# Graph network on one core: gate terms in column quarters, a reordered last finish, a later transpose

## The chip, the cores and the metric

The kernel runs on one core of one Trainium2 chip. The metric is device time in microseconds (us): the median of the runs of one launch. A core has a matrix engine (TensorE, in the profile PE, its weight loads PEld), a vector engine (VectorE, DVE), a scalar engine (ScalarE, ACT), GpSimd (POOL) and a queue that only issues transfers (SyncE, SP). Every engine takes its own instructions in order, and semaphores tie the engines together. TensorE writes its results to PSUM, which has 8 banks here; everything else lies in SBUF or in DRAM.

## The reference

A graph of 2708 nodes with 512 features each, an adjacency matrix `adj` (2708 x 2708), and four layers, each ending with `x = layernorm(x + layer(x))`. What matters for the change are the gates of layer 1 and the whole of layer 3:

```python
# layer 1: two gates per node, each from the summed and the own features
type_sum = adj @ x
attn_a = sigmoid(concatenate([type_sum, x], 1) @ Wa.T + ba)   # one number per node
attn_b = sigmoid(concatenate([type_sum, x], 1) @ Wb.T + bb)
x_b = adj @ (x @ W_gcnb) + b_gcnb                              # = type_sum @ W_gcnb + b_gcnb
...
x = layernorm(x + sigmoid(attn_a * x_a + attn_b * x_b))
# layer 2: out = x @ w0 + A x @ w1 + A^2 x @ w2 + A^3 x @ w3, worked out in three hops
# layer 3, with deg the count of neighbours
a_norm = deg**-0.5 * (adj + eye) * deg**-0.5
x = layernorm(x + relu((a_norm @ x + x) @ W + b))
```

All is float32. In this program one float32 matrix product of 128 rows by 128 columns appears in the profile as two matmul instructions, called passes here.

## The kernel before

The product of the adjacency with the features is done seven times (one "sweep" each: layer 0, the two products of layer 1, the three hops of layer 2, layer 3). Each sweep forms 2 x 2 blocks with seven products instead of eight (Strassen's scheme in Winograd's form), so VectorE adds and subtracts blocks of adjacency and features ahead of TensorE, and adds products from PSUM into tiles of results behind it. The results lie transposed: features on the 128 partitions, nodes along the free dimension. `C[h, c]` (layers 0 and 1) or `cc(s, c)` (layers 2 and 3) is such a tile: half `h` of the nodes, a quarter `c` of the features (`DC` = 4 quarters of 128 features). In the sweeps of layers 0 and 1 the nodes of a half are cut into four ranges of 384, 384, 256 and 330 nodes (`RANGES`); in the others into two ranges of two parts each, `s` = 0 and 1, of 338 or 339 nodes (`RANGES2`).

The order of the work is written as a list of events. `at(pos, fn)` puts a piece of work at a position, and the list is sorted by position and emitted (L1344); a scheduler of the framework then places the instructions on the engines, mostly in that order, and adds the semaphores. An event made with `hold=True` is tied to stay behind what stands before it on its engine. In layer 1 one position unit is one product of a range: 10 blocks of 128 rows for two column halves, 40 passes. In the last sweeps two position units are seven products (`u = 2 / 7`).

Behind each completed range a "finish" runs between the matmuls of the next product:

- `done1` (L912), layer 1, called once for each half of each range, 8 times in all, with `p0` the position of its start. For each tile of up to 128 nodes (22 in all: 20 of 128, two of 74) event `b` first takes the two gate terms: four matmuls with 128 nodes of `C` as weights and the 128 x 2 gate weights `wab_sb` as moving data (L917), an addition on VectorE (L919), a sigmoid on ScalarE (L920). Then come the dense product with `W[1]` (helper `dense`, L586, 8 passes of 512 columns), the bias, the gate and the store.
- `done5` (L1263), the third hop of layer 2: `b` turns a tile of nodes back with TensorE (L1232), normalises it (`layernorm`, L539) and stores it; `c`, 0.85 positions later, turns the normalised tile once more (L581), ScalarE copies it from PSUM into one of two `xT` tiles (L583), and GpSimd stores it (L601) for layer 3.
- `done6` (L1298), layer 3, called for two ranges and two halves. `pre(s, c)` (L1310) does three VectorE operations over a whole part of results (L1313 to L1315), which need a row of degrees (`rows`, L1299) and a tile from DRAM (`load_x3T`, L1305). Then for each of the 6 tiles of nodes `a` fetches the node's features (`fetch2`, GpSimd's queue, into one of the 6 `nat` tiles) and `b` does the dense product, bias and relu (L1332, L1333), the layernorm and the store. The last of the four calls is range 1, half 0, which ends the kernel.

`layernorm` goes from engine to engine: statistics on VectorE (L541, L543, L545), a power on GpSimd (L546), a product on VectorE (L548), the scaling on ScalarE (L551). GpSimd also issues most of the loads and stores of features, in the same queue as its powers. The adjacency, the row tiles, the degree rows and the `x3T` tiles share one ring of 38 tiles of SBUF (`RING`).

Where the last 84 rows of both halves are multiplied (`rest`, L456 and L1201), the kernel already cuts the array into four groups of 32 rows and runs four matmuls of 32 rows each, one in every group (L468, L1210).

Of the kernel before, what the change touches and what calls it, by code (L numbers as in the profile page):

```python
# [21 lines left out]
F32 = mybir.dt.float32  # L22
BF = mybir.dt.bfloat16
AF = mybir.ActivationFunctionType
ALU = mybir.AluOpType
P = 128
# [42 lines left out]
def gnn_kernel(ctx: ExitStack, tc: tile.TileContext, x, adjT, w_sa, a_sa, w_gcn, b_gcn, wab, bab, w_hop, w_out,  # L69
# [32 lines left out]
    nc.vector.memset(rdeg, 1.0)  # L102
    wab_sb = const.tile([P, 2 * DC, 2], F32, name="wab_sb")
    bab_sb = const.tile([P, 2], F32, name="bab_sb")
    vmat = const.tile([P, DC, 4], F32, name="vmat")
# [647 lines left out]
    def start0():  # L753
# [10 lines left out]
        for c in range(DC):  # L764
            nc.vector.tensor_copy(vmat[:, c, 2:4], wab_sb[:, DC + c, :])

    def x0_load(k, s):
# [22 lines left out]
    W = {}  # L790
# [120 lines left out]

    def done1(p0, dp, last, R0, n, h, C, tiles):  # L912
        for i, (t, lo, w) in enumerate(tiles):
            def b(t=t, lo=lo, w=w):
                pz = bank("pz", [P, 2])
                for c in range(DC):
                    nc.tensor.matmul(pz[:w], C[h, c][:, lo : lo + w], wab_sb[:, c, :], start=c == 0,  # L917
                                     stop=c == DC - 1)
                nc.vector.tensor_tensor(gate[:w, t, :], pz[:w], gate_x[:w, t, :], ALU.add)  # L919
                nc.scalar.activation(gate[:w, t, :], gate[:w, t, :], AF.Sigmoid)  # L920
                px = dense(lambda c: C[h, c][:, lo : lo + w], W[1], w)
                y = nat("y")
                nc.vector.tensor_tensor(y[:w], px[:w], vec[1][:w], ALU.add)
                nc.scalar.mul(y[:w], y[:w], gate[:w, t, 1:2])
                move(nc.gpsimd, XB[t], y[:w])

            at(p0 + 0.25 + dp * i, b)
# [335 lines left out]
    def done5(p0, dp, g, i0, n, h, cc, tiles):  # L1263
        for i, (s, lo, w) in enumerate(tiles):
# [13 lines left out]
            at(p, b)  # L1278
            at(p + 0.85, c)

# [17 lines left out]
    def done6(p0, dp, g, i0, n, h, cc, tiles):  # L1298
# [4 lines left out]
        x3T = {}  # L1303

        def load_x3T(s, c):  # L1305
            t = ring_tile("x3T")
# [10 lines left out]
        for s in range(2):  # L1317
            at(p0 - 0.6, lambda s=s: rows(s))
            for c in range(DC):
                at(p0 - 0.5 + 0.4 * s + 0.05 * c, lambda s=s, c=c: load_x3T(s, c))  # L1320
                at(p0 + 0.4 * s + 0.05 * c, lambda s=s, c=c: pre(s, c), True)
        for i, (s, lo, w) in enumerate(tiles):
            got = {}
# [12 lines left out]

            p = p0 + 0.4 + (0.25 if dp > 0.13 else 0.15) * i
            at(p - 0.6, a)
# [58 lines left out]
```

## Time and profile before

| | |
|---|---|
| device time, median of 3 | 2927.45 us (2926.04 to 2929.18) |
| span of the profiled execution | 2926.3 us |
| TensorE busy | 98% of the span |
| VectorE busy | 76% |
| ScalarE, GpSimd busy | 20%, 23% |
| share of the chain that ended last: TensorE | 84% |
| the gate terms, `pz` L917 | from 519.8 to 897 us |
| second transposes of the last range of hop 3, `ps_t` L581 | 2521.6 to 2541.8 us |
| last matmul of the sweep of layer 3, then the last finish | 2892.6 us to the end |

In the timeline a row has the start, the duration, the engine, the line, the operation with its output and inputs, the weights' and the moving operand's shapes, a count of merged instructions and, in brackets, how long the engine was idle before and what ended that. Durations of matmuls overlap each other, because they are pipelined: what one costs is read from the distance of the starts. So the share of TensorE's busy time says that there is hardly any gap, and the gaps themselves are read in the table of waits.

### The profile page before, as it was taken

The page shows a single profiled execution, that of the slowest core. Times are in us where ns is not written, and L with a number is a line of the kernel's source. Part 1 is how long each engine was busy: PE and PEld are TensorE (multiplying, and loading weights), DVE is VectorE, ACT ScalarE, POOL GpSimd, SP SyncE. Part 2 cuts the span into 40 slices and gives each one's busy share as a digit, 9 for nine tenths or more (in the row PEclk, how much of TensorE's full clock was granted, in tenths as well). Part 3 has the DMA queues.
Part 4 walks back from the last instruction along what each step waited for, and adds up shares of the span by engine and source line. Part 5 has one row for each costly group of instructions (what it writes and reads, how often), then busy time and mean ns, then how long its engine had stood idle before and what let it go on. Part 6 is the DMA issues. An engine that isn't in the chain of part 4 may idle for free.

```text
span 2926.3 us, 37538 instructions
## 1 busy us (share of the span) xinstructions
PE 2866.8 (98%) x10914; PEld 1856.8 (63%) x10914; DVE 2234.4 (76%) x5667; ACT 571.5 (20%) x1121; POOL 661.3 (23%) x1178
## 2 busy tenths in 40 slices
PE   7999999999999999999999999999999999999998
PEld 5655665557765656866666666666666666665664
DVE  5898797666656675775789788887888878689886
ACT  4544200000145454651100000000000201101001
POOL 0133224213310101123213033030330413512212
PEclk9999999999999999999999999999999999999999
DMA  7666476444544333564667667576775766866652
GB/s 224 187 212 180 133 224 215 131 153 150 173 128 131 115 116 97 169 196 149 207 205 222 203 201 233 160 215 197 217 223 148 229 200 184 240 181 182 180 163 87
DMA packets 376250, 523.99 MB, mean 179 GB/s; under 512 B 64454, under 2 KB 326640, under 8 KB 376044
## 3 DMA queue, kind: packets, MB, share of 16 engines
q1 hardware_dynamic: 305688, 370.70, 43.4%
q0 software_dynamic: 53376, 139.76, 14.7%
q10 hardware_dynamic: 16980, 11.13, 1.3%
q8 instruction: 87, 1.43, 0.2%
q14 instruction: 119, 0.97, 0.1%
HBM read 432.14 MB, written 89.21 MB: 178 GB/s over the span
## 4 chain that ended last, share of the span: by engine, by line
PE 84%; DVE 6%; issue 4%; DMA 3%; POOL 1%; SPq 1%; ACT 0%; POOLq 0%; DVEq 0%; ACTq 0%
PE accu L1135 11%; PE accd L1135 11%; PE accc L1135 11%; PE ps_d L592 9%; PE accd L444 9%; PE accu L444 8%; PE accc L444 8%; PE acca L1135 5%; PE acca L444 4%; PE accr L1206 2%; DVE z L1095 1%; PE accr L1210 1%; PE accd L453 1%; PE ps_t L581 1%; PE pz L917 1%
## 5 line engine op out<-in xcount | busy, mean ns | idle before, releaser
L1095 DVE TENSOR_TENSOR z<-z 128x339 f32<-128x339 f32 (+1 forms) x966 | 456.3, 503 | 13.5 <-PE accu L1135 2.5
L1153 ACT COPY q<-accu 128x338 f32<-128x338 f32 (+1 forms) x84 | 34.3, 444 | 994.5 <-PE accu L1135 836.0
L1135 PE MATMUL accc<-s,t 128*128 128x338 f32 (+1 forms) x644 | 200.1, 455 | 0.0
L1135 PE MATMUL accu<-z,t 128*128 128x338 f32 (+1 forms) x644 | 194.9, 448 | 1.6 <-DVE q L1159 1.6
L1135 PE MATMUL accc<-z,t 128*128 128x338 f32 (+1 forms) x644 | 194.4, 448 | 0.0
L1135 PE MATMUL accd<-z,t 128*128 128x338 f32 (+1 forms) x644 | 193.6, 448 | 0.0
L546 POOL TENSOR_TENSOR rstd<-rstd,neg_half 128x1 f32<-128x1 f32 (+3 forms) x92 | 62.2, 676 | 579.3 <-DVE rstd L545 578.6
L1256 POOL DMA_DIRECT2D Y<-y x192 | 105.1, 554 | 373.6 <-DVE y L1251 344.2
L389 DVE TENSOR_TENSOR a<-a,a 128x384 f32<-128x384 f32 (+2 forms) x330 | 161.3, 509 | 19.5 <-PE accu L444 18.6
L1135 PEld LDWEIGHTS accc<-s,t 128*128 128x128 f32 x644 | 122.1, 192 | 65.9 <-issue 10.3
L1135 PEld LDWEIGHTS accd<-z,t 128*128 128x128 f32 x644 | 122.2, 190 | 61.3 <-issue 1.7
L1135 PEld LDWEIGHTS accu<-z,t 128*128 128x128 f32 x644 | 121.4, 190 | 62.0 <-DVE q L1159 2.1
L1135 PEld LDWEIGHTS accc<-z,t 128*128 128x128 f32 x644 | 121.7, 190 | 60.9 <-issue 2.2
L1095 DVE TENSOR_TENSOR s<-z 128x338 f32<-128x338 f32 (+1 forms) x322 | 150.0, 503 | 10.6 <-PE accc L1135 6.2
L1159 DVE TENSOR_TENSOR q<-q,accd 128x338 f32<-128x338 f32 (+1 forms) x112 | 56.2, 502 | 132.4 <-PE accd L1135 132.3
L953 ACT ACTIVATE e<-row,neg_s 128x384 f32<-128x384 f32 (+5 forms) x176 | 100.4, 571 | 89.9 <-DVE e L955 28.2
L955 DVE TENSOR_TENSOR e<-e,f 128x384 f32<-128x384 f32 (+5 forms) x176 | 87.3, 504 | 23.8 <-ACT f L954 23.0
L954 ACT ACTIVATE f<-row,neg_s 128x384 f32<-128x384 f32 (+5 forms) x176 | 100.1, 568 | 25.5 <-PE accc L444 6.2
L882 DVE SCALAR_TENSOR_TENSOR deg<-a,deg 128x384 f32<-128x384 f32 (+2 forms) x152 | 74.0, 502 | 30.8 <-DMA a<-in_adjT 30.2
L592 PE MATMUL ps_d<-w,q 128*128 128x512 f32 (+2 forms) x192 | 86.4, 595 | 4.7 <-DVE q L1315 3.4
L392 POOL DMA_DIRECT2D As<-a x120 | 65.0, 544 | 111.5 <-DVE a L389 103.6
L956 DVE SCALAR_TENSOR_TENSOR a<-a,e 128x384 f32<-128x384 f32 (+2 forms) x160 | 80.0, 506 | 3.7 <-DMA a<-in_adjT 1.3
(602 smaller groups left out, 5934.9 us busy)
## 6 DMA issues: line engine op xcount, KB each, us to landing
z<-As SPq DMA_DIRECT2D x320, 169.5 KB
z<-As SPq DMA_DIRECT2D x320, 169.0 KB
a<-in_adjT SPq DMA_DIRECT2D x240, 192.0 KB
z<-in_adjT SPq DMA_DIRECT2D x240, 169.5 KB
z<-in_adjT SPq DMA_DIRECT2D x240, 169.0 KB
a<-in_adjT SPq DMA_DIRECT2D x120, 165.0 KB
a<-in_adjT SPq DMA_DIRECT2D x112, 128.0 KB
As<-a POOLq DMA_DIRECT2D x60, 192.0 KB, 3.4
```

What stands on the lines that cost most here:

```text
L389: nc.vector.tensor_tensor(A[r, dst, k][:, :n], A[r, a, k][:, :n], A[r, b, k][:, :n], op)
L392: nc.gpsimd.dma_start(out=SD[m][k * P : (k + 1) * P, R0 : R0 + n], in_=A[r, dst, k][:, :n])
L444: nc.tensor.matmul(B[home, c][:, :n], X[STAT[p], k][:, c * P : (c + 1) * P], A[r, MOV[p], k][:, :n], start=bool(start and k == k0), stop=k ...
L592: nc.tensor.matmul(o, lhs(c), r, start=c == 0 and n == 0, stop=c == DC - 1, skip_group_check=True)
L882: nc.vector.scalar_tensor_tensor(d[:w, :n], a[:w, :n], 0.0, d[:w, :n], ALU.not_equal, ALU.add)
L953: nc.scalar.activation(e[:w, :n], row[R0, h][0][:w, :n], AF.Exp, bias=neg_s[:w, t : t + 1])
L954: nc.scalar.activation(f[:w, :n], row[R0, h][1][:w, :n], AF.Exp, bias=neg_s01[:w, t : t + 1])
L955: nc.vector.tensor_tensor(e[:w, :n], e[:w, :n], f[:w, :n], ALU.min)
L956: nc.vector.scalar_tensor_tensor(a[:w, :n], a[:w, :n], 0.0, e[:w, :n], ALU.not_equal, ALU.mult)
L1095: nc.vector.tensor_tensor(d[:, :n], Z[x + (k,)][:, :n], Z[y + (k,)][:, :n], op)
L1135: nc.tensor.matmul(B[home][:, :n], stat(v, k), a[:, :n], start=bool(start and k == 0), stop=k == nk - 1, skip_group_check=True)
L1256: nc.gpsimd.dma_start(out=rows[:, :, f * P : (f + 1) * P], in_=o[32 * f : 32 * (f + 1), : m * P].rearrange("p (b d) -> p b d", d=P))
```

## The change

There are three parts.

1. Gates of a range at once. Per call of `done1`, four matmuls take the four feature quarters of the whole range as moving data, each with 32 columns of weights (`wab_pad`, of which two are not zero), and each writes another group of 32 partitions of one bank `pg`: four quarters of the array's columns. ScalarE copies the bank into a tile `zg` of the ring. For each tile of nodes one matmul with 128 columns of `zg` as weights and a 128 x 2 matrix `pick` of zeros and ones adds the four quarters up. It comes after the dense product instead of before it, and the tiles of a range share one bank `pz`. `wab_pad` and `pick` are filled once.
2. In `done5` the second transpose comes 1.1 instead of 0.85 positions after the first.
3. In the last call of `done6` rows, loads and the `pre` work start earlier, during the last product (the features `c` >= 2, which are complete first, ahead of the others; part 1 ahead of part 0), the three tiles of part 1 come ahead of those of part 0, and the first dense product stands directly behind the last matmul of the sweep instead of 0.5 positions later. It is meant to let TensorE go on without waiting for the last results.

```diff
+    wab_pad = const.tile([P, DC, 32], F32, name="wab_pad")
+    nc.vector.memset(wab_pad, 0.0)
+    pick = const.tile([P, 2], F32, name="pick")
+    nc.vector.tensor_copy(pick, ident[:, 0:2])
+    for c in range(1, DC):
+        nc.vector.tensor_tensor(pick, pick, ident[:, 32 * c : 32 * c + 2], ALU.add)
...
+            nc.vector.tensor_copy(wab_pad[:, c, 0:2], wab_sb[:, c, :])
...
     def done1(p0, dp, last, R0, n, h, C, tiles):
+        Z = {}
+
+        def gates():
+
+            pg = bank("pg")
+            for c in range(DC):
+                nc.tensor.matmul(pg[32 * c : 32 * c + 32, :n], wab_pad[:, c, :], C[h, c][:, :n], start=True, stop=True)
+            Z[0] = trans("zg")
+            nc.scalar.copy(Z[0][:, :n], pg[:, :n])
+
+        at(p0 + 0.05, gates)
         for i, (t, lo, w) in enumerate(tiles):
-            def b(t=t, lo=lo, w=w):
-                pz = bank("pz", [P, 2])
-                for c in range(DC):
-                    nc.tensor.matmul(pz[:w], C[h, c][:, lo : lo + w], wab_sb[:, c, :], start=c == 0,
-                                     stop=c == DC - 1)
+            def b(i=i, t=t, lo=lo, w=w):
+                px = dense(lambda c: C[h, c][:, lo : lo + w], W[1], w)
+                if i == 0:
+                    Z[1] = bank("pz", [P, 8])
+                pz = Z[1][:, 2 * i : 2 * i + 2]
+                nc.tensor.matmul(pz[:w], Z[0][:, lo : lo + w], pick, start=i == 0, stop=True, skip_group_check=True)
                 nc.vector.tensor_tensor(gate[:w, t, :], pz[:w], gate_x[:w, t, :], ALU.add)
                 nc.scalar.activation(gate[:w, t, :], gate[:w, t, :], AF.Sigmoid)
-                px = dense(lambda c: C[h, c][:, lo : lo + w], W[1], w)
...
-            at(p + 0.85, c)
+            at(p + 1.1, c)
...
+        end = (g, h) == (1, 0)
...
-            at(p0 - 0.6, lambda s=s: rows(s))
+            at(p0 - (1.9 if end else 0.6), lambda s=s: rows(s))
             for c in range(DC):
-                at(p0 - 0.5 + 0.4 * s + 0.05 * c, lambda s=s, c=c: load_x3T(s, c))
-                at(p0 + 0.4 * s + 0.05 * c, lambda s=s, c=c: pre(s, c), True)
-        for i, (s, lo, w) in enumerate(tiles):
+                if end:
+                    a = p0 - 1.8 + 0.05 * c
+                    b = p0 - 1.5 + 0.2 * (c - 2) + 0.4 * s if c >= 2 else p0 + {
+                        (1, 1): -0.9, (1, 0): -0.6, (0, 1): -0.3, (0, 0): -0.07}[s, c]
+                else:
+                    a, b = p0 - 0.5 + 0.4 * s + 0.05 * c, p0 + 0.4 * s + 0.05 * c
+                at(a, lambda s=s, c=c: load_x3T(s, c))
+                at(b, lambda s=s, c=c: pre(s, c), True)
+        for i, (s, lo, w) in enumerate(tiles[3:] + tiles[:3] if end else tiles):
...
-            p = p0 + 0.4 + (0.25 if dp > 0.13 else 0.15) * i
+            p = p0 - 0.095 + 0.14 * i if end else p0 + 0.4 + 0.25 * i
             at(p - 0.6, a)
             at(p, b)
```

## The prediction

> **What bounds the kernel now.** I began with the page, to see which engine fills the span.
>
> ```profile
> PE 2866.8 (98%) x10914; PEld 1856.8 (63%) x10914; DVE 2234.4 (76%) x5667; ACT 571.5 (20%) x1121; POOL 661.3 (23%) x1178
> ```
>
> TensorE is idle for only 2926.3 - 2866.8 = 59.5 us. So there are two ways to gain: fewer passes, or one of these few gaps. Next I asked who TensorE waits for while layer 1 makes its gates (480 to 910 us):
>
> ```profile
> PE ps_r L840 <- DVE rcol L835: 1.3, 1, 1.3
> ```
>
> This is the whole answer: in these 430 us TensorE is the bound, and a pass taken away there shortens the kernel by its length. Its timeline gives the lengths:
>
> ```profile
> 512.07 0.59 PE L468 MATMUL accc<-r,B22R 32*128 32x384 f32 x2
> 512.08 0.59 PE L468 MATMUL accu<-r,B22R 32*128 32x384 f32 x2
> 512.49 0.49 PE L468 MATMUL accc<-r,B22R 32*128 32x384 f32 x2
> 512.50 0.49 PE L468 MATMUL accu<-r,B22R 32*128 32x384 f32 x2
> 512.92 4.14 PE L444 MATMUL accd<-a,B22A 128*128 128x384 f32 x12
> 516.90 0.72 PE L896 MATMUL ds<-ones_f,deg 128*128 128x1 f32 x6
> ...
> 520.15 0.50 PE L917 MATMUL pz<-wab_sb,C 128*128 128x2 f32 x4
> 520.51 0.59 PE L917 MATMUL pz<-wab_sb,W 128*128 128x2 f32 x4
> 520.96 1.96 PE L592 MATMUL ps_d<-w,C 128*128 128x512 f32 x4
> 522.76 1.88 PE L592 MATMUL ps_d<-w,W 128*128 128x512 f32 x4
> 524.47 2.74 PE L444 MATMUL accd<-a,B22C 128*128 128x384 f32 x8
> 527.05 0.50 PE L917 MATMUL pz<-wab_sb,C 128*128 128x2 f32 x4
> ```
>
> Starts count, not durations. The last two rows: 8 passes of 384 columns take 2.58 us. A tile's gates and dense product take 524.47 - 520.15 = 4.32 us; a dense product alone takes 3.43 (so in the chain of waits), hence a tile's gates 0.89, 0.11 for each of their 8 passes of only two columns. The L468 rows are four matmuls on row quarters, two passes each: all four first passes start within 0.01 us, all second ones 0.42 later.
>
> Then the end. TensorE from the last product on:
>
> ```profile
> 2891.30 1.30 PE L1135 MATMUL acca<-z,B21D 128*128 128x339 f32 x4
> 2894.84 13.14 PE L592 MATMUL ps_d<-w,q 128*128 128x512 f32 x30 [2.24 <-DVE q L1315]
> 2908.87 3.70 PE L592 MATMUL ps_d<-w,q 128*128 128x512 f32 x8 [0.89 <-DVE q L1315]
> 2912.83 4.56 PE L592 MATMUL ps_d<-w,q 128*128 128x512 f32 x10 [0.27 <-DVE q L1315]
> ```
>
> Three times it waits for `pre`. VectorE's waits from 2839 to 2893 us, and the busy times (PE, PEld, DVE, ACT, POOL) of the last 23 us of the sweep:
>
> ```profile
> DVE rstd L548 <- POOL rstd L546: 8.8, 6, 4.4
> ```
>
> ```profile
> 2870.00:2880.00 10.00, 9.34 (x33) 5.89 (x31) 4.16 (x12) 1.53 (x2) 6.10 (x12) 1.00 0.48 138
> 2880.00:2893.00 13.00, 11.67 (x40) 7.52 (x40) 7.06 (x17) 0.09 (x1) 4.86 (x10) 1.00 0.41 125
> ```
>
> VectorE has room (11.2 of 23 us used), but once stands 4.4 us behind a GpSimd power, itself queued behind a fetch that waits for a `nat` tile. Last, the one wait of the transposes:
>
> ```profile
> 2539.95 0.59 ACT L583 COPY xT<-ps_t 128x512 f32<-128x512 f32 x1 [5.61 <-DMA X3T<-xT]
> 2540.43 0.78 ACT L551 ACTIVATE o<-ps_n,rstd 83x512 f32<-83x512 f32 x1
> 2541.26 0.51 PE L581 MATMUL ps_t<-ident,o 83*128 83x83 f32 x4 [4.26 <-ACT o L551]
> ```
>
> **What the Trainium skill says.** "TensorE: Matmul & The Clock Gate", "Packing small matmuls — row/col tiling": matmuls of 32 columns in distinct column groups run concurrently; three of them with 512 columns gained 2.38x, about like row groups. The trace shows row groups only (2.58 us of passes in 0.85). The same page, "LDWEIGHTS": a load costs by its columns, P / 1.2 ns, 107 ns for 128; the 0.11 us per gate pass agrees, so these passes are bounded by their weights. "TensorEngine Tiling (Array Packing)", "Key Properties": changing the tiling mode drains the array. The trace agrees, with little: the 8 passes ahead of 512.07 start at 509.39 and end at 509.39 + 2.58 = 511.97, so 0.10 is lost, and after it the 12 passes to 516.90 take 3.98 instead of 3.87, another 0.11. The first page's table says that VectorE and GpSimd take strict turns; the 4.4 us above are such a case.
>
> **Part 1, the gates.** Removed: 20 tiles at 0.89 and two of 74 nodes at 0.54 (864.67 to 868.64, less 3.43), together 18.9 us. Added per call: four quarter matmuls. Their nearest row is L468: 0.85 + 0.10 + 0.11 = 1.06 us at 384 nodes; at 330 nodes 0.77 (862.69 to 863.46) + 0.2 = 0.97; at 256 nodes two passes of 0.215 and the same overhead, 1.06 - 0.645 = 0.415, make 0.85. With four, two and two calls: 4.2 + 1.9 + 1.7 = 7.9 us. No row shows column quarters, so the other bound is one after the other: 8 passes each, 4 x 2.58 + 2 x 2.22 + 2 x 1.72 = 18.2 us (the 2.22 and 1.72 are 8 passes at 330 and 256 columns, 850.39 to 852.61 and 751.83 to 753.55). I take 7.9: the weights, 32 columns, load faster, and the skill puts both kinds level. Added per tile: the `pick` matmul, two passes bounded by their weights, 22 x 2 x 0.11 = 4.9 us. Net: 18.9 - 7.9 - 4.9 = 6.1 gained; one after the other 4.2 lost.
>
> The added waits. The gates stand 8 passes behind the end of their product and need VectorE's additions (L505). Those end at 515.29 where the gates' turn comes at 512.92 + 0.11 + 2.58 = 515.61; at 558.67 against 558.92 for the other half; nearly level for 256 nodes (744.44 against 744.47). Queued behind on TensorE is the whole next product, so I charge 0.1 in all: 6.0. ScalarE's copy (0.5 us, 8 times) has 3.4 us of dense product before the first `pick` needs it, on an engine that had been idle 13.95 us before a gate. The gate's addition now delays `y` by some 0.3 us, but nothing on TensorE waits for `y`. One ring tile more for some 15 us leaves 37; the trace shows no wait of TensorE for a load here. Filling `wab_pad` and `pick` costs nothing: VectorE idles from 1.3 to 3.49 us until the first adjacency lands, and `ident` is ready at 1.31.
>
> **Part 2, the transpose.** 0.25 positions are 0.25 / u = 0.875 products of 2.85 us: 2.5 us of matmuls go ahead. The wait of 4.26 us then shrinks by 2.5 if ScalarE's order stays, more if the scaling L551 overtakes the copy L583, which itself waits for an `xT` tile. VectorE's L548 for it was done at 2539.3, so 2540.2 is its earliest turn instead of 2541.26: up to 3.6. I take 3.0 (0 to 3.6). A `nat` tile is held 2.5 us longer; six tiles of nodes have six of them.
>
> **Part 3, the finish.** Work is the same, its place is not. The sweep's passes end at 2891.30 + 4 x 0.285 = 2892.4; six dense products, 48 passes of 0.429, take 20.6. Without waits they end at 2913.0, before at 2912.83 + 10 x 0.429 = 2917.1: 4.1 us. From there the end took 9.2 us. The last tile's L1333 started at 2919.06 and not at 2918.3, its L548 at 2922.17 behind another tile's power, both because two tiles had bunched up: 1.4 us that even spacing (2.4 us of VectorE per 3.43 us of TensorE) saves. Sum 5.5. Against it: seven of eight `pre` (1.52 us each, 2893.18 to 2900.8 for five) move into the sweep. VectorE then needs 11.2 + 10.6 = 21.8 of 23 us, and a wait like the 4.4 no longer fits. The additions that TensorE's last product needs ended at 2885.8; they may slip by three `pre`, 4.5 us, past their use from 2889.6 on. I charge 1.0. Bounds: 7.1 gained, if the stall of 1.6 us at 2880.9, an heir of the 4.4, goes too, and a loss of 4.4 if another such wait lands on TensorE. Ring: ten tiles earlier, but after them only five loads follow. I take 4.5.
>
> Sum: 6.0 + 3.0 + 4.5 = 13.5, so 2927.45 - 13.5 = 2914.
>
> **The rivals.**
> - The column quarters run one after another. For it: no trace of this case shows them, and float32 makes two passes of each. Against it: the row quarters. -4.2 + 3.0 + 4.5 = 3.3 gained: 2924. Chance 0.17.
> - The finish gains nothing, because VectorE becomes the bound of the last product. For it: 21.8 of 23 us. Against it: most of what moves may lag without TensorE noticing. 9 gained: 2918.5. Chance 0.24.
> - Slower: quarters one after another (4.2 lost), no gain from the transpose, and loads issued earlier on GpSimd's queue put one more wait of 4.4 us before TensorE: 2936. For it: fetches and powers share that queue, as the 8.8 us show. Against it: three things would have to fail together. Chance 0.07.
>
> **How the numbers follow.** My forecast, 2914, has 0.52. The bound of 0.2% is 5.9 us, so the forecast and the second rival are faster, the first rival is no change, with a little of it on either side: faster 0.77, same 0.17, slower 0.06. The range runs from 2905 (6.1 + 3.6 + 7.1 = 16.8 gained would be 2910.7; some 6 us more for a queue order that nobody can read off) to 2924 (the first rival).
>
> **What would show it.** Four `pg` passes starting within 0.02 us and the next four some 0.4 us later, about 1.06 us to the next full pass; with starts 0.32 us apart the first rival holds. `pick` passes costing 0.22 a tile. The wait of L581 under 2 us. No wait of `ps_d` for L1315 in the last 30 us, and the last dense pass within 21 us of the last sweep pass. Wrong I would be if L1135 showed new waits for VectorE after 2870 us, or if the scheduler's new order moved waits into sweeps that the change doesn't touch.

## The result, and the profile after

The changed kernel takes 2924.24 us in the median of 4 runs (2920.08 to 2927.5), the kernel before 2928.31 us beside it (2926.04 to 2931.68). The ratio is 0.9984, with a 95% interval of 0.9965 to 1.0004: about 4 us gained where I had predicted 13.5, and a time just above the end of my range, 2924. The profile after is that of a run of 2927.24 us, 3 us over the median of its four, the one before that of a run of 2928.07 us. So the parts went the way I had forecast for one of them only. The line numbers of the changed kernel: the sweep's matmuls are L1154 (before L1135), its additions of blocks of the adjacency L1114 (L1095), of features L1135 (L1116), the additions behind it L1178 (L1159), ScalarE's copies of first results L1172 (L1153), the power L553 (L546), the dense product L599 (L592), `pre` ends in L1336 (L1315). In kernels without part 1 they are L1143, L1103, L1124, L1167 and L1161.

The first part of the page after:

```profile
PE 2863.2 (98%) x10846; PEld 1844.0 (63%) x10846; DVE 2234.8 (76%) x5676; ACT 578.9 (20%) x1133; POOL 658.1 (22%) x1178
```

TensorE has 68 instructions fewer and is busy 3.6 us less. Its idle time is 2925.2 - 2863.2 = 62.0 us, 2.5 more than before: what the passes gave, waits took back in part.

To see where, I laid the two traces over each other. The n-th pass into an accumulator in one kernel belongs to the n-th in the other, and the difference of their starts changes only where time is won or lost. Positions are those of the kernel before; a minus is time won.

| stretch of the kernel before | after minus before, at its end | won or lost in it |
|---|---|---|
| layer 0, to 505 us | +4.1 | +4.1 |
| gates, to 989 us | -3.9 | -8.0 |
| rest of layer 1, to 1410 us | -1.6 | +2.3 |
| hops of layer 2, to 2490 us | -1.9 | -0.3 |
| transposes and start of layer 3, to 2602 us | -0.6 | +1.3 |
| layer 3, to 2870 us | -0.6 | 0.0 |
| its last product, to 2892 us | +4.1 | +4.7 |
| the last finish, to the end | -1.1 | -5.2 |

The first row has hardly anything to do with the change: up to 505 us TensorE has the same instructions in the same order in both kernels, and VectorE has them too but for nine small ones that fill `wab_pad` and `pick`. At this point the sixteen experiments, which fill both as well, stood from -1.6 to +4.5 against this one profile of the kernel before. Steps of 1 to 2 us near 1326 or 1540 us, as in the third row, appear in the experiments that change nothing there, too (e7: 1.69 at 1326 us; e6: 1.67 near 1540 us). So a single profile tells a stretch from another one to 2 us at best, while the stretches of the gates repeat within 0.5 us, as will be seen.

**Part 1.** The timeline of TensorE after, at the first call:

```profile
517.00 2.85 PE L451 MATMUL accd<-a,B22A 128*128 128x384 f32 x8
519.78 0.52 PE L927 MATMUL pg<-C,wab_pad 128*32 128x384 f32 x2
519.79 0.52 PE L927 MATMUL pg<-W,wab_pad 128*32 128x384 f32 x2
520.13 0.49 PE L927 MATMUL pg<-C,wab_pad 128*32 128x384 f32 x2
520.14 0.49 PE L927 MATMUL pg<-W,wab_pad 128*32 128x384 f32 x2
520.56 1.56 PE L451 MATMUL accd<-a,B22A 128*128 128x384 f32 x4
521.96 0.72 PE L904 MATMUL ds<-ones_f,deg 128*128 128x1 f32 x6
...
525.21 1.88 PE L599 MATMUL ps_d<-w,C 128*128 128x512 f32 x4
526.92 1.88 PE L599 MATMUL ps_d<-w,W 128*128 128x512 f32 x4
528.64 0.28 PE L938 MATMUL pz<-pick,zg 128*128 128x2 f32 x2
528.78 2.83 PE L451 MATMUL accd<-a,B22C 128*128 128x384 f32 x8
531.44 1.88 PE L599 MATMUL ps_d<-w,C 128*128 128x512 f32 x4
```

Four passes start within 0.01 us, the other four 0.35 later: the column quarters run side by side. The next full pass stands 0.78 us behind. What a call costs in all is read from the same twelve passes of 384 columns in both kernels: with the call between them they take 521.96 - 517.00 = 4.96 us, before 516.90 - 512.92 = 3.98 (the rows are in the prediction). So a call costs 0.98 us, the 0.78 and 0.1 on either side for the change of mode. Behind a `pick` the next pass starts 0.14 us later, but the eight passes after it take 531.44 - 528.78 = 2.66 us instead of 2.58; from tile to tile 531.44 - 525.21 = 6.23 us stand against 527.05 - 520.15 = 6.90 before, so a tile saves 0.67 of the 0.89 us of its old gates, and its `pick` costs 0.22.

**Part 2.** TensorE's waits after, from 2515 to 2680 us:

```profile
PE accu L1154 <- DVE z L1114: 3.0, 1, 3.0
PE accd L1154 <- DVE z L1114: 2.3, 2, 1.3
...
PE accc L1154 <- ACT q L1172: 0.3, 1, 0.3
```

The 4.26 us of the transpose are gone. In their place TensorE waits for additions of blocks of the adjacency, and VectorE in turn for a load:

```profile
2546.17 0.43 DVE L1135 TENSOR_TENSOR t<-B11D,B11B 128x256 f32<-128x256 f32 x1 [6.57 <-DMA B11D<-X]
```

These are features of layer 3, the output of hop 3 that was stored to DRAM some microseconds ago. Before, VectorE did the same sum at 2549.66, but TensorE stood in its stall in the meantime, and so the reload cost nothing.

**Part 3.** TensorE's timeline after, the last product and the finish:

```profile
2882.93 4.81 PE L1154 MATMUL accu<-z,t 128*128 128x339 f32 x10 [4.17 <-DVE q L1178]
2887.57 3.01 PE L1154 MATMUL accc<-z,t 128*128 128x339 f32 x10
...
2896.84 20.87 PE L599 MATMUL ps_d<-w,q 128*128 128x512 f32 x48
```

The 48 dense passes run without a gap, as I had counted. Ahead of them TensorE waits 4.17 us where it had waited 1.59, and the ten passes after this wait take 4.64 us instead of 2.85. What VectorE waited for, from 2835 us to the end:

```profile
DVE rstd L555 <- POOL rstd L553: 15.2, 12, 3.5
```

15.2 us for powers of GpSimd; it was 11.2 before, and 10.0 to 13.6 in the nine experiments whose last finish is that of the kernel before.

The ten slow passes are the clock. Here are windows before (the wait of the transpose ends at 2541.26) and then after; the number behind the engines' busy times is the granted clock:

```profile
2541.00:2545.00 4.00, 3.74 (x11) 2.51 (x12) 1.15 (x3) 1.14 (x3) 3.64 (x7) 0.62 0.53 143
```

```profile
2882.00:2886.00 4.00, 3.07 (x8) 1.94 (x9) 3.93 (x11) 0.09 (x1) 1.09 (x3) 0.76 0.66 183
```

The Trainium skill, "TensorE: Matmul & The Clock Gate", "What's actually happening", says that an idle window of about 3.4 us puts TensorE on half its clock until it has been busy for such a window again, and that the windows run freely. The traces agree in part. After a wait of about 4 us some six passes start 0.56 us apart instead of 0.285, a slow stretch of 3.4 us, which costs 1.7 us more. But a wait need not last a whole such window: after one of 3.0 us this happened in the changed kernel and not in e2, after one of 2.24 us in e1 and not in the kernel before. Here the measurement decides: shorter waits can lower the clock as well. So the wait of the transpose had been worth 4.26 + 1.7 = 6.0 us, and the 4.17 us after cost as much.

### The profile page after: what moved, and what is told of

It reads as the page before. It is cut to its first block, busy times and chain, and to the rows that moved or that the text cites. A ratio compares the mean times of both kernels' runs of the same rounds, so it can differ in the third digit from the quotient of the medians.

```text
span 2925.2 us, 37394 instructions
## 1 busy us (share of the span) xinstructions
PE 2863.2 (98%) x10846; PEld 1844.0 (63%) x10846; DVE 2234.8 (76%) x5676; ACT 578.9 (20%) x1133; POOL 658.1 (22%) x1178
## 5 line engine op out<-in xcount | busy, mean ns | idle before, releaser
L1114 DVE TENSOR_TENSOR z<-z 128x339 f32<-128x339 f32 (+1 forms) x966 | 455.9, 502 | 15.5 <-PE accu L1154 3.6
L1172 ACT COPY q<-accu 128x338 f32<-128x338 f32 (+1 forms) x84 | 34.5, 443 | 984.2 <-PE accu L1154 984.2
L1154 PE MATMUL accu<-z,t 128*128 128x338 f32 (+1 forms) x644 | 196.5, 452 | 7.2 <-DVE q L1178 4.2
L1154 PE MATMUL accc<-s,t 128*128 128x338 f32 (+1 forms) x644 | 198.5, 451 | 0.4 <-DVE s L1114 0.4
L1154 PE MATMUL accc<-z,t 128*128 128x338 f32 (+1 forms) x644 | 196.1, 451 | 0.3 <-ACT q L1172 0.3
L1154 PE MATMUL accd<-z,t 128*128 128x338 f32 (+1 forms) x644 | 193.8, 448 | 1.3 <-DVE z L1114 1.3
L553 POOL TENSOR_TENSOR rstd<-rstd,neg_half 128x1 f32<-128x1 f32 (+3 forms) x92 | 62.0, 674 | 581.7 <-DVE rstd L552 581.1
L1154 PEld LDWEIGHTS accu<-z,t 128*128 128x128 f32 x644 | 122.3, 191 | 69.5 <-DVE q L1178 4.7
L1154 PEld LDWEIGHTS accc<-z,t 128*128 128x128 f32 x644 | 122.7, 192 | 62.5 <-issue 3.9
L1154 PEld LDWEIGHTS accc<-s,t 128*128 128x128 f32 x644 | 120.7, 190 | 64.9 <-issue 8.7
L1154 PEld LDWEIGHTS accd<-z,t 128*128 128x128 f32 x644 | 122.0, 190 | 62.7 <-DVE z L1114 1.9
L1114 DVE TENSOR_TENSOR s<-z 128x338 f32<-128x338 f32 (+1 forms) x322 | 150.0, 502 | 11.7 <-PE accc L1154 7.5
L1178 DVE TENSOR_TENSOR q<-q,accd 128x338 f32<-128x338 f32 (+1 forms) x112 | 56.1, 501 | 128.0 <-PE accd L1154 128.0
L599 PE MATMUL ps_d<-w,q 128*128 128x512 f32 (+2 forms) x192 | 86.0, 595 | 1.4 <-DVE ld L1360 1.3
```

Source lines behind the costliest of these rows:

```text
L553: nc.gpsimd.tensor_tensor(rstd[:w, 1:2], rstd[:w, 0:1], neg_half[:w], ALU.pow)
L599: nc.tensor.matmul(o, lhs(c), r, start=c == 0 and n == 0, stop=c == DC - 1, skip_group_check=True)
L1114: nc.vector.tensor_tensor(d[:, :n], Z[x + (k,)][:, :n], Z[y + (k,)][:, :n], op)
L1154: nc.tensor.matmul(B[home][:, :n], stat(v, k), a[:, :n], start=bool(start and k == 0), stop=k == nk - 1, skip_group_check=True)
```

## The experiments

My theory after the comparison: part 1 does what was forecast; part 2 trades the transpose's wait for the reload of features; part 3 trades the gaps of the finish for waits behind GpSimd's queue. Rivals: in part 2 some other limit at the start of layer 3, in part 3 VectorE's own work in the last product. Each experiment is compared with the runs of the kernel before that were taken beside it on the same chip.

### e1 to e3: each part alone

The diff is the change's own, cut to one part (the constants `wab_pad` and `pick` stay in all of them).

e1, the gates alone.

> Part 1 alone. Theory (four column quarters run at once, TensorE bound): between 510 and 910 us TensorE comes out 6.5 to 8 us earlier than before against its own start of that stretch; nothing else moves; 2921 +- 3. Rival (the gates' new waits for VectorE, or the changed order of its queue, give the gain back in the second product of layer 1): TensorE is again where it was by 1400 us; 2927.

e2, the transpose alone.

> Part 2 alone. Theory (the removed wait is replaced by one further back: VectorE's sums of blocks wait for the load of features just stored): the wait of the second transpose (4.3 us) is gone, VectorE waits 5 to 7 us for B11D, TensorE 4 to 6 us for z; at the end of that product TensorE stands 0 to 1.5 us later than before; time 2928 to 2929. Rival (the transpose's wait was worth its length, the loss seen belongs to the gates): 3 to 4 us earlier, 2924.

e3, the finish alone.

> Part 3 alone. Both theories: the stretch from the last sweep pass to the end is 5 us shorter, and TensorE loses 4 to 5 us before it (a wait of 4 us for VectorE's q before the accu product, and ten passes at half pace); time within 1 us of before, 2927 to 2928. If the loss is missing, it came from the place where the gates or the transposes had shifted the last sweep to: then 2922.

| | us | ratio, 95% interval | in its own stretch |
|---|---|---|---|
| e1 gates | 2924.28 | 0.9986 (0.9979 to 0.9992) | -8.1, from +2.0 at 505 to -6.1 at 989 us |
| e2 transpose | 2931.48 | 1.0011 (1.0003 to 1.002) | 0.0: -5.9 at 2541, and back by 2577 us |
| e3 finish | 2931.1 | 1.0005 (0.9996 to 1.0014) | +4.7 in the last product, then -5.6 |

Part 1 gains, part 2 alone makes the kernel slower by some 0.1%, part 3 changes nothing that can be told. The stretch of the gates was worth between 7.8 and 8.3 us in all seven kernels with part 1 (the changed one, e1, e4, e11, e12, e15, e16). Why e1 gains only some 4 us in the median when its stretch gives 8 is not fully settled. In its profile 2.0 us of the difference stand in layer 0, where next to nothing differs and single profiles wander; a small cost of the two constants can't be told from that. Another 1.7 us stand in the last finish, whose 30 dense passes follow a wait of 2.24 us in both kernels:

```profile
2889.91 14.84 PE L599 MATMUL ps_d<-w,q 128*128 128x512 f32 x30 [2.24 <-DVE q L1336]
```

Before, the same 30 took 13.14 us. In e1 four of them start 0.85 us apart instead of 0.43, and so in e2, e5, e6, e10 and e14; in e7, e8, e9 and e13 they don't. This is the clock again, and no part of the change.

What follows the transpose's wait in e2, TensorE's waits from 2515 to 2680 us:

```profile
PE accu L1143 <- DVE z L1103: 3.0, 1, 3.0
PE accd L1143 <- DVE z L1103: 2.0, 3, 1.2
...
PE accc L1143 <- ACT q L1161: 1.3, 1, 1.3
```

### e5: are the column quarters what makes part 1 pay?

Part 1 alone, but the four matmuls accumulate into the same 32 partitions, so they must follow one another; `pick` becomes the first two columns of the identity, ScalarE copies 32 rows, and VectorE fills the whole of `zg` with zeros ahead of that.

```diff
-                nc.tensor.matmul(pg[32 * c : 32 * c + 32, :n], wab_pad[:, c, :], C[h, c][:, :n], start=True, stop=True)
+                nc.tensor.matmul(pg[:32, :n], wab_pad[:, c, :], C[h, c][:, :n], start=c == 0, stop=c == DC - 1)
```

> Part 1 alone, but the four gate matmuls of a range accumulate in one and the same column group (the other 96 rows of zg are set to zero by VectorE). If the quarters of the change really run at once, each call now costs TensorE 2.6 us at 384 nodes instead of 1.0, over the 8 calls 10 us more than with four groups, and TensorE is 3 to 4 us later than before by 910 us. If the quarters had not been at once, the cost stays as it was.

One run: 2941.98 us, beside 2936.04 of the kernel before on the same chip. TensorE's timeline:

```profile
516.40 1.48 PE L925 MATMUL pg<-C,wab_pad 128*32 128x384 f32 x4
517.71 1.45 PE L925 MATMUL pg<-W,wab_pad 128*32 128x384 f32 x4
519.10 1.56 PE L449 MATMUL accd<-a,B22A 128*128 128x384 f32 x4
```

2.70 us from the first of them to the next full pass, against 0.78. The stretch loses 9.5 us, from +0.7 at 505 to +10.2 at 989 us, where the quarters win 8.1; 4.1 of it is a new wait of 2.4 us for VectorE's additions at 780 us, with slow passes behind it, and VectorE's filling of `zg` may have a part in that. The rest is a loss too, so without the quarters part 1 would not pay, as my first rival had it.

### e4, e6, e11: whose wait is it in the last product?

e4 has parts 1 and 3, the transpose at 0.85, and in the last call rows, `x3T` loads and fetches are issued by SyncE.

```diff
-            nc.gpsimd.dma_start(out=row[g, h, s][:, :n], in_=bcast(DROW[h][0:1, i0 + s * n : i0 + (s + 1) * n], n))
+            (nc.sync if end else nc.gpsimd).dma_start(out=row[g, h, s][:, :n], in_=bcast(DROW[h][0:1, i0 + s * n : i0 + (s + 1) * n], n))
...
-            nc.gpsimd.dma_start(out=t[:, :n], in_=X3T[g, h, s][c * P : (c + 1) * P, :])
+            (nc.sync if end else nc.gpsimd).dma_start(out=t[:, :n], in_=X3T[g, h, s][c * P : (c + 1) * P, :])
...
-                got["x"] = fetch2(X3, h, r0, w)
+                got["x"] = fetch2(X3, h, r0, w, nc.sync if end else nc.gpsimd)
```

> Parts 1 and 3, the transpose as before, and the last finish's loads (degree rows, x3T, fetched features) on SyncE's queue instead of GpSimd's. Theory A (those loads, and fetches that wait for a free tile, stand in front of GpSimd's powers, so VectorE waits for a power and TensorE for VectorE): VectorE's waits for powers in the last 60 us of the sweep fall from 10 us to under 4, TensorE's wait before the accu product falls from 4.2 to under 1, and the time is 7 + 5 + 1.5 us below before, 2914 to 2916. Theory B (VectorE has too much to do, because the pre work lies in the last product): TensorE still loses 3 to 4 us there; 2918 to 2920.

e6 has nothing but the earlier loads of part 3, on GpSimd's queue as in the change; `pre` and the tiles stay where the kernel before has them.

```diff
-            at(p0 - 0.6, lambda s=s: rows(s))
+            at(p0 - (1.9 if end else 0.6), lambda s=s: rows(s))
...
-                at(p0 - 0.5 + 0.4 * s + 0.05 * c, lambda s=s, c=c: load_x3T(s, c))
+                at(p0 - 1.8 + 0.05 * c if end else p0 - 0.5 + 0.4 * s + 0.05 * c, lambda s=s, c=c: load_x3T(s, c))
```

> Of part 3 only the earlier degree rows and x3T loads of the last call, on GpSimd's queue; pre work, order of tiles and dense products as before. Theory A (loads in front of the powers): TensorE's wait before the accu product of the last sweep grows from 1.6 to 3 to 4 us, though no pre work lies there. Theory B (the pre work itself): it stays at 1.6, and the fetches that were in the queue before are the only ones that powers wait for.

e11 is e4 with the fetches left on GpSimd's queue.

```diff
-                got["x"] = fetch2(X3, h, r0, w, nc.sync if end else nc.gpsimd)
+                got["x"] = fetch2(X3, h, r0, w)
```

> Parts 1 and 3, transpose at 0.85; of the last finish only the rows and x3T loads are issued by SyncE, the fetches of node features stay on GpSimd's queue. If the earlier loads (0.56 to 1.2 us each in GpSimd's queue) hold the powers: no wait of TensorE before its last product, as with all of them on SyncE, and 2916 to 2918 us beside 2916.6 of that. If the fetches that wait for a nat tile hold them: TensorE's wait of about 4 us before the last product stays, and the time is 2920 to 2922 us.

| | us | ratio, 95% interval | last product | VectorE's wait for powers from 2835 us |
|---|---|---|---|---|
| before | 2928.31 | 1 | 0 | 11.2 |
| after | 2924.24 | 0.9984 (0.9965 to 1.0004) | +4.7 | 15.2 |
| e6 | 2938.09, beside 2936.04, one run | - | +3.8 | 12.6 |
| e11 | 2920.68 | 0.9974 (0.9964 to 0.9984) | +1.1 | 11.7 |
| e4 | 2916.6 | 0.9957 (0.9942 to 0.9972) | -1.9 | 7.3 |

The waits of TensorE from 2835 us in e6, where only loads were moved, up to the last finish:

```profile
PE accu L1143 <- DVE q L1167: 3.8, 1, 3.8
```

And in e4 VectorE's, in a kernel whose TensorE has no wait left in these 90 us:

```profile
DVE rstd L555 <- POOL rstd L553: 7.3, 12, 0.7
```

```profile
2885.85 20.76 PE L599 MATMUL ps_d<-w,q 128*128 128x512 f32 x48
```

So the wait is GpSimd's queue: it goes with the loads and fetches although all eight `pre` stay where the change put them (e4, and in the same way e12, e15 and e16 below, with 1.8 to 1.9 us won in the last product). VectorE's own work, my rival, has room. With the loads away alone 3.6 of the 4.7 us go (e11), with the fetches, which wait for a `nat` tile, another 3.0, more than the rest of the 4.7. How one of them stands before a power, in GpSimd's timeline after:

```profile
2878.82 0.54 POOL L145 DMA_DIRECT2D ld<-X  x1 [1.84 <-DMA z<-in_adjT]
2879.36 0.56 POOL L1328 DMA_DIRECT2D x3T<-X3T  x1
2879.91 0.51 POOL L147 DMA_DIRECT2D ld<-X  x1
2880.44 0.56 POOL L553 TENSOR_TENSOR rstd<-rstd,neg_half 83x1 f32<-83x1 f32 x1
```

VectorE, its statistics done at 2877.2, took one block addition more and then stood until the power's end at 2881.0, and the blocks and results that TensorE needed next stood behind.

That the earlier loads make this wait is not shown, though e6 looks like it. Nine experiments leave the last finish as it was before. Four of them (e1, e2, e5, e14) lose nothing in the last product, and five (e7, e8, e9, e10, e13) lose 4.1 to 5.3 us, without a load moved; in e7, e8 and e13 every engine has the instructions of the kernel before, in its order, from 2690 us on. TensorE and GpSimd in e7:

```profile
2883.23 4.70 PE L1143 MATMUL accu<-z,t 128*128 128x339 f32 x10 [4.01 <-DVE q L1167]
```

```profile
2879.10 0.52 POOL L145 DMA_DIRECT2D ld<-X  x1 [3.31 <-DMA out<-ld]
2879.61 1.10 POOL L1317 DMA_DIRECT2D x3T<-X3T  x2
2880.73 0.58 POOL L553 TENSOR_TENSOR rstd<-rstd,neg_half 83x1 f32<-83x1 f32 x1
```

The kernel before has the same fetch ahead of the same power, only 2.3 us earlier, at 2876.80 and 2878.43 us. So it can fall into this wait itself, and how much of the 4.7 us is the change's stays open. What makes the difference between the four and the five does too.

### e7, e8: is it the reload that takes part 2's gain?

Both let six of layer 3's feature tiles come from `X2`, long stored, and not from `X3`; their output is thus not the network's, but no sum has to wait for a fresh store. e7 has the transpose at 0.85, e8 at 1.1.

```diff
-    next_x2(S[6], X3)
+    next_x2(S[6], [X2[t] if KT // 2 <= t < KT else X3[t] for t in range(NT)])
```

> The transpose as before (0.85), gates and finish as before, but the sweep of layer 3 loads its features of rows 640 to 1354 of the first half from the result of layer 1 (finished long ago) instead of the result of layer 2, so that it need not wait for the last normalised tiles (its output is not the reference's). It is the yardstick for the next run: the transpose's wait of 4.3 us should still be there or be a little shorter, and VectorE's wait for B11D be short.

> The later transpose (1.1) with the same other source of features. Theory (the stored features set the time): with the dependence gone, TensorE keeps what the later transpose saves and stands 3 to 4 us earlier at the end of that product than in the yardstick. Rival (VectorE is late for another reason, such as its order or too much work there): TensorE still waits 4 to 6 us for z, as in the run of the transpose alone.

e7 took 2932.01 us and e8 2934.07, beside 2936.04 of the kernel before, one run each. In e7 TensorE wins 5.8 us from 2490 to 2602 us with the transpose where it was: the wait of 4.26 us goes with the reload. Two things are seen from that. First, the wait had a reload behind it, in GpSimd's timeline before:

```profile
2536.37 0.55 POOL L138 DMA_DIRECT2D B11C<-X  x1 [2.59 <-DMA X<-o]
2536.91 1.10 POOL L138 DMA_DIRECT2D X<-o  x2
2538.00 0.52 POOL L140 DMA_DIRECT2D X<-o  x1
2538.54 0.57 POOL L546 TENSOR_TENSOR rstd<-rstd,neg_half 83x1 f32<-83x1 f32 x1
```

A load that waits for its store stood ahead of the last tile's power. That is what the Trainium skill, "DMA: Bandwidth & Descriptors", "Anatomy of one DMA — SWDGE (gpsimd) path", says of any such wait: it is kept by the sequencer that issues, the transfer engines don't wait. Here it cost the instructions behind it 2.6 us. It was not alone: VectorE's product behind this power was done at 2539.30 us, and the copy L583, which stood ahead of the scaling on ScalarE and waited for the store of its tile until 2539.95 (in the prediction), ended last. In e7 the scaling comes ahead of such a copy, so e7 removes both and doesn't part them. Second, e8 lost its waits for VectorE's blocks (0.6 us left of 5.0), but gained only 1.4, because of a new one:

```profile
PE accc L1143 <- ACT q L1161: 3.7, 1, 3.7
```

ScalarE's copy of results stood in its queue behind a copy into an `xT` tile, which waited 5.95 us for that tile's store. There are two `xT` tiles. Two dependencies were now suspected, not one.

### e9, e10: a third xT tile

e9 is part 2 alone, e10 is e8, each with three `xT` tiles; there was room only with one ring tile less.

```diff
-RING = 38
+RING = 37
...
-        t = pool.tile([P, DC, P], F32, name="xT", tag="xT", bufs=2)
+        t = pool.tile([P, DC, P], F32, name="xT", tag="xT", bufs=3)
```

> Part 2 alone, with three xT tiles instead of two (and one ring tile less, 37). My theory: two dependencies stand behind the transpose. ScalarE's copies of results (q) stand in its queue behind copies into xT that wait for an xT tile to be stored, and VectorE's sums of features wait for the load of features of layer 3 that were just stored. The third tile takes the first one away alone: TensorE's wait for ScalarE's q (1.25 us with part 2 alone) goes, its waits for VectorE's z (3.0 and 2.0) stay; TensorE stands 1 to 2 us ahead of the kernel before at 2674 us, against level with two tiles. Rival: the tiles alone were to blame; then the z waits go as well and TensorE stands 4 to 6 us ahead there.

> Part 2 alone with three xT tiles and with part of layer 3's sweep reading the features of layer 1 in place of those just stored (so the result is not that of the network; only the dependency is taken away). My theory: with both dependencies gone nothing is left to take the place of the transpose's wait: no wait of TensorE over 1.5 us between 2522 and 2674 us, and TensorE 5 to 6 us ahead of the kernel before at 2674 us. Rival: a third resource holds the start of layer 3; then another wait of 2 us or more shows and under 3 us are gained.

2939.39 and 2944.91 us, beside 2927.59. Neither settles anything of part 2: the missing ring tile brought its own waits, 3.4 and 3.0 us of TensorE for blocks already at 2504 us, and in e10 VectorE then stood for the adjacency, from 2515 to 2690 us:

```profile
DVE z L1103 <- DMA z<-in_adjT: 7.4, 1, 7.4
```

I had not reckoned with the ring: one tile of 38 fewer costs TensorE 3 us at this one place.

### e13: both dependencies away, the ring untouched

e8 with the first copies of results at the start of layer 3 made by VectorE instead of ScalarE (again not the network's output).

```diff
-                        nc.scalar.copy(Q[dst, p, c][:, :n], B[home][:, :n])
+                        (nc.vector.tensor_copy if dve else nc.scalar.copy)(Q[dst, p, c][:, :n], B[home][:, :n])
```

`dve` is true for the first three products of layer 3.

> Part 2 alone, with part of layer 3's sweep reading the features of layer 1 in place of those just stored (so the result is not that of the network), and with the first copies of results of layer 3 made by VectorE instead of ScalarE, so that they do not stand behind the copies into xT; two xT tiles and 38 ring tiles as in the kernel before. If the reload of features and ScalarE's queue are all that took the place of the transpose's wait: no wait of TensorE for ScalarE's q, none over 1.5 us for VectorE's z between 2535 and 2680 us, and TensorE 4 to 6 us ahead at 2674 us of where it was at 2520 us, against the kernel before. Rival: something else holds the start of layer 3; then waits of 3 us or more in sum stay.

One run, 2929.81 us beside 2928.68. All waits of TensorE from 2535 to 2680 us:

```profile
PE ps_d L599 <- DVE ld L1349: 1.3, 1, 1.3
PE accr L1214 <- DVE q L1225: 0.4, 1, 0.4
```

No wait for `z`, none for `q`; from +2.4 at 2490 to -5.1 at 2602 us it wins 7.6. So these two are all that took the place of the transpose's wait. The 7.6 are not the later transpose's alone: the other source by itself, with the transpose at 0.85, had won 5.8 (e7), so that the later place is worth some 2 us at most on top of it. (In the last product, where this kernel is the kernel before, it loses 5.0 us, one of the five cases above.)

### e14, e15, e16: can a queue give it back?

The stores of the last range's transposed tiles go from GpSimd's queue to ScalarE's: e14 with part 2 alone, e15 with all parts and e4's queues, e16 as e15 with the transpose at 0.85. e12 is e15 without this edit, that is, the change with e4's queues.

```diff
     def store_T(dst, xT, queue=nc.gpsimd):
-        nc.gpsimd.dma_start(out=dst.rearrange("(c p) i -> p c i", p=P), in_=xT)
+        queue.dma_start(out=dst.rearrange("(c p) i -> p c i", p=P), in_=xT)
```

> All three parts, and the rows, loads and fetches of the last finish issued by SyncE. If the later transpose costs what it cost alone (ratio 1.0011): about 3 us more than without it, 2919 to 2920 us. If it gains 3 us here, as I had predicted: 2913 to 2914 us. The powers of GpSimd: VectorE's wait for them from 2835 us on under 9 us in all, as without part 2.

> Part 2 alone, with the stores of the transposed tiles of the last range of hop 3 issued by ScalarE, right behind its copies, instead of by GpSimd. If GpSimd's queue (0.8 us for each such store, and its wait for the copy) delays the reload of features: the second load into B11D is issued 1 to 3 us earlier after its features are scaled, TensorE's wait of 3.0 us for VectorE's z shrinks to under 1.5 us, and the time is 1 to 3 us under that of the kernel before. If the reload's own flight (5.5 us) sets it: the waits stay at about 5 us in sum and the ratio stays at 1.001.

> All three parts, the last finish's loads and fetches issued by SyncE, and the stores of the last range's transposes issued by ScalarE. If GpSimd's queue is what costs the later transpose its gain: 2913 to 2916 us (2919.6 without the second change). If the flight of the reload sets it: 2918 to 2920 us.

> Parts 1 and 3, the transpose at 0.85, the last finish's loads and fetches issued by SyncE, and the stores of the last range's transposes issued by ScalarE. The transpose's wait of about 4 us is set by the layernorm of the last tile, whose power stands in GpSimd's queue: with 0.8 us per store less there I expect it 1 to 2 us shorter, 2915 to 2917 us, beside 2916.6 without the last change. If the queue is not what sets it: 2916 to 2918 us and the wait stays.

| | transpose | stores by | us | ratio, 95% interval | 2490 to 2602 us |
|---|---|---|---|---|---|
| e4 | 0.85 | GpSimd | 2916.6 | 0.9957 (0.9942 to 0.9972) | +0.6 |
| e12 | 1.1 | GpSimd | 2919.61 | 0.9971 (0.996 to 0.9982) | +3.9 |
| e14 (without parts 1, 3) | 1.1 | ScalarE | 2938.39 | 1.0038 (1.0025 to 1.0051) | +1.2 |
| e15 | 1.1 | ScalarE | 2919.71 | 0.9971 (0.9961 to 0.9981) | -0.9 |
| e16 | 0.85 | ScalarE | 2926.32 | 0.9993 (0.9984 to 1.0001) | +6.2 |

e12 against e4 says that the later transpose loses with the finish repaired, too: 3.2 us in its stretch, 4 us by the ratios, though the intervals overlap. Moving the stores is no remedy as it stands: e15's ratio is e12's although its stretch is better by 4.8 us, and e14 and e16 are slower than their partners e2 and e4. Much of this is lost at the very end. From the issue of the last store to the end 9.0 us pass in e14, 6.7 in e15 and 7.0 in e16, in all other kernels 2.5 to 2.9. What lasts is GpSimd's closing drain, first in e14, then in e4 (shortest, median and longest of three, in ns):

```profile
L1409 POOLq DRAIN  x3: 51/98/10302, 2929.1 to 2939.9; - x3
```

```profile
L1420 POOLq DRAIN  x3: 46/98/1565, 2909.4 to 2913.9; - x3
```

Together with the stretches in the table this gives a difference of -0.9 us for e15 against e12 (0.1 in the medians), 9.9 for e16 against e4 (9.7) and 7.6 for e14 against e2 (6.9). Why the drain is longer with these stores on ScalarE's queue is not shown. Among kernels with that edit the later transpose is the better one (e15 against e16, 6.6 us), so what it is worth depends on what else stands in these queues.

In e14, GpSimd's timeline shows the second half of the reload waiting for the store of the features itself, though no transposed store is in that queue any more:

```profile
2544.42 0.59 POOL L145 DMA_DIRECT2D B11D<-X  x1 [0.55 <-DMA X<-o]
2549.58 0.55 POOL L145 DMA_DIRECT2D B11D<-X  x1 [4.58 <-DMA X<-o]
```

The store was under way for up to 6.3 us and the load 5.4 more. In the kernel before these were up to 4.4 and 3.8 us in the median: from 2541 to 2545 us its TensorE crept and the transfer engines were busy for 0.53 of the time (the next to last number of the window above), where the changed kernel keeps them at 1.02 from 2540 to 2545 us. Whether the fuller transfer engines lengthen the flight was not tried by itself. e16 I had wrong outright: it lost 6.2 us with VectorE 10.6 us at the same reload, and why there and not in e15 is open.

## Why the prediction was wrong

- **TensorE as the bound of the gates, and part 1's 6.0 us: right**, somewhat low. The stretch gave 8.0, of which 6.9 are passes. Column quarters ran side by side, and a call costs 0.98 us at 384 nodes where the working from row quarters had 1.06, all eight some 7.2 and not 7.9. A `pick` costs the 0.22 us a tile that I had taken. The other 1.1 are the wait of `ps_r` for `rcol`, which fell from 1.3 to 0.2 us; in kernels without part 1 it lies between 0 and 1.7, so this is not shown to be the change's. I had charged 0.1 for new waits; there were none.
- **Part 2, "I take 3.0 (0 to 3.6)": wrong, and the step that failed is the one that costs the wait by what shortens it alone.** It asked when `o` would be ready and stopped there. The transpose's wait did go, and it had been worth 6.0 us with the slow passes behind it, not 4.26. But the next limits lay just behind it: features stored and loaded again, which VectorE's sums need, and copies on ScalarE behind two `xT` tiles. The trace of before had both, `DMA X<-o` releasing a `B11C<-X` and the copy L583 waiting 5.61 us, the latter in a line that I showed. Measured: 1.3 us lost in the changed kernel, 0.0 in e2, 3.2 lost between e4 and e12; with both limits away 7.6 won (e13), of which 5.8 need no later transpose (e7).
- **Part 3, "I charge 1.0": the mechanism of the finish was right, this term was mis-sized.** The finish gave 5.2 us after (5.5 predicted). The charge measured 4.7, and it was not VectorE's crowding by `pre`, as I had argued from 21.8 of 23 us, but GpSimd's queue: fetches held by `nat` tiles, and loads of 0.5 to 0.6 us each, ahead of the powers. I had taken the 1.59 us that one profile shows there for what this place costs, but five of nine kernels with the old finish lose 4.1 to 5.3 us more in it, so a part of the 4.7 may be chance. I had the case in hand as the bound of -4.4 and as part of the rival that ends slower, and gave it too little weight; it came without the quarters failing. With the queue relieved, both terms together gave 7.5 us (e4: from -4.7 at 2870 us to 12.2 at the end of the profiles), a little more than my upper bound of 7.1.
- **The rivals.** The first one's time, 2924, was met, but not its way: the quarters aren't serial (e5 shows what it would have cost). The second had the right place, the last product, and the wrong engine.
- **The range**: its upper end was the first rival alone. It left out that the transpose gains nothing and another wait lands on TensorE while the quarters work: with my own numbers 6.0 + 0 + 5.5 - 4.4 = 7.1, so 2920, and a wait that comes back in part 2 goes on top, as it did.

e4 is the version to keep: gates in column quarters, the reordered finish, the transpose left at 0.85, and the last loads issued by SyncE: 2916.6 us, 0.43% under the kernel before, its four runs (2915.96 to 2919.08) all below the four of the changed kernel.

## What to carry to other kernels

When a wait is to be removed, look up what the waiting engine needs next and when that comes; a store that is read back and a pair of buffers that must be emptied both run in the shadow of the wait and surface when it goes. A queue that issues transfers and also computes makes every transfer's wait a wait of the computation behind it: move transfers that wait for buffers to a queue with nothing behind them before putting them earlier. A wait of TensorE long enough to lower its clock costs more than its length, here 1.7 us on 4.2. And before a difference at one place is put down to the change, look at the same place in the runs that leave it alone: in the last product they differed by 5 us among themselves.

## What the runs showed of the hardware that I had not expected

- Four matmuls of 32 columns by 384, on four column quarters, take 0.78 us in two passes each, where one group takes 2.70 for the same passes (e5).
- Passes after a wait of about 4 us run at half pace for some 3.4 us (starts 0.56 apart, granted clock 0.62 to 0.76 over 4 us). After shorter waits it varies: after one of 3.0 us they did so in the changed kernel and not in e2 or e12, after one of 2.24 us in e1 and not in the kernel before, after one of 1.88 us in e15.
- A `pick` of two two-column passes costs 0.22 us, as much as two of the old gates' passes at 0.11, although the pass behind it starts only 0.14 us later: the rest is seen in the eight passes that follow.
- With twelve more stores issued by ScalarE instead of GpSimd, GpSimd's closing drain took 7.9 to 10.3 us (e14 to e16) instead of 1.5 to 3.9.
